# A graph network on one core: new order and timing of the first loads, and x1 + z·h summed ahead of the candidate state in five groups instead of two

## The chip, the cores and the metric

The kernel runs on one core of a Trainium2 chip. A core has a matrix engine (TensorE, PE in the profile; its weight loads are listed apart as PEld), a vector engine (VectorE, DVE), a scalar engine (ScalarE, ACT), GpSimd (POOL) and SyncE (SP), which here issues the DMAs. Each engine runs its instructions in program order and waits on semaphores for the others. The metric is the time of one execution on the device, in microseconds. Before the change it was 2103.77 us, the median of three runs (2102.31 to 2104.01).

## The reference

128 graphs have 128 nodes each, with 256 features per node. Each graph has its adjacency matrix of integers. Two residual layers follow one another; cut to what matters:

```python
# layer 0: three rounds of a gated graph convolution
h = maximum(layernorm(x), 0)
A = (adj != 0)
for i in range(3):
    m = h @ weight[i]                       # [b, n, 256]
    aggr = einsum('bst,bsd->btd', A, m)     # sums over edges
    gi = aggr @ w_ih.T + b_ih;  gh = h @ w_hh.T + b_hh
    r = sigmoid(i_r + h_r);  z = sigmoid(i_z + h_z)
    n = tanh(i_n + r * h_n)                 # the candidate state
    h = (1 - z) * n + z * h
x = x + h
# layer 1: attention over the edges
h = maximum(layernorm(x), 0)
Wh = h @ W;  s = Wh.sum(-1)
e = where(adj == 0, -inf, leaky_relu(s_i + s_j, 0.2))
x = x + softmax(e) @ Wh
```

## The kernel before, in words

The graphs are worked in 32 groups of four (G = 4, NG = 32). A group passes four stages: normalization, and then the three rounds ("layers" 0, 1, 2) of the gated convolution; behind layer 2 follows its attention. In layers 0 and 1 the state is held transposed (hT: features on the partitions); in layer 2 it is held by rows (rows: nodes on the partitions), because the result is added to x, which is kept by rows in the buffer x1.

The product with weight[i] is folded into w_ih ahead of time: the kernel multiplies each weight[i] by w_ih once, at the start (L449, "compose"), so that a round needs only the sum over edges of h (buffer aT) and one product of it. For this w_ih, w_hh and weight are loaded and turned on PE (L351 for w_ih and w_hh, L438 for weight), copied from PSUM to SBUF by DVE and ACT (L358), and their block sums are made (L369 to L377), since the large products use a scheme with seven block multiplications in place of eight. That scheme gives the PSUM banks their names: x_rz, x_n, y_rz, y_n, q_rz, q_n, one bank of each, and two more called misc. The lines L693 and L700 are its matmuls, L732 and L736 to L738 the ACT copies that empty an x or y bank, L725 the ACT copies that seed one, and L742 the DVE additions that read a q bank. A bank is free for its next product only when its copy is done.

The program isn't written in the order in which it runs. Every operation is recorded in a plan (function op) with its engine, an estimated duration, what it reads and writes, a due time and a lag (the time the plan allows from its end until another engine can use the result; 3300 ns for a load). A list scheduler (Plan.run) then ranks the operations by due time, follows clocks for the five engines, and gives out one fixed order for each engine. The operations of PE that belong to the products form a chain of fixed order. The whole is laid out in 96 turns, one for each group and layer, one turn every 18150 ns of planned time (SLOT); in the middle of the kernel each period of three turns takes group g through layer 0, group g−1 through layer 1 and group g−2 through layer 2. The last twelve turns have an order of their own, written out by hand: (29,0), (30,0), (28,1), (27,2), (31,0), (29,1), (28,2), (30,1), (31,1), (29,2), (30,2), (31,2). Because due times and estimated durations decide the order, an edit of one of them can move operations that it doesn't name.

What the change touches:

- L313 to L318: before the planned work, PE runs matmuls of the identity matrix into the banks y_rz and y_n (L315). They write the banks once and are PE's first work. The identity itself is made by POOL (masks.py:197 and 199).
- load (L332 to L334): one DMA on SP's queue, with a lag of 3300 ns. The planner knows no bandwidth of its own: a load costs its size times a constant.
- weights (L387 to L402 and on): the loads of w_ih in two halves of 384 KB (L394 to L397), of weight[0] (load_msg(0), 256 KB), w_hh (768 KB), weight[1] and the biases, each with a due time that ranks it among SP's other issues. In the profile w_ih and w_hh are called rz, since they lie in buffers of that name, and the weights of a layer are called e.
- group (L901 to L906): the loads of a group's rows (512 KB) and adjacency (at, 256 KB). For the first four groups (TIMED = 4) they go through load; later ones are planned with a small fixed cost. L907 turns at into a mask on DVE; L500 to L512 are the statistics of a normalization and L516 its relu on ACT; L530 turns h on PE.
- gru_rows (L819 to L882), the gated update of layer 2. The group's rows are done in two halves. With rz holding tanh(./2), so that z = (rz + 1)/2, a half normally does: the tanh of u on ACT (L855), d = rows − u on DVE (L873), x1 += u on POOL (L875), d = (rz + 1)·d on DVE (L878), and x1 += d/2 on DVE (L881). For the last EARLY_Z groups it does instead, with the same result: d = (rz + 1)·rows (L859) and x1 += d/2 (L862) on DVE, which don't need the candidate state; then the tanh (L855), u = (rz − 1)·u (L865) and x1 −= u/2 (L868), both on DVE. Before, EARLY_Z is 2: groups 30 and 31.

Of the kernel before, what the change touches and what calls it, by code (L numbers as in the profile page):

```python
# [9 lines left out]
BF16 = mybir.dt.bfloat16  # L10
# [6 lines left out]
P = 128  # L17
# [4 lines left out]
WHOLE = 1  # L22
EARLY = 3
ENDING = 2
EARLY_Z = 2
SLOT = 18150
MARGIN = 7000
TIMED = 4
KB = 3
# [12 lines left out]
class Plan:  # L42
# [14 lines left out]
    def buf(self, tag):  # L57
        n, kind = self.tags[tag]
        if kind == "free" or kind == "turn":
            b = Buf(tag, tag, None)  # L60
            if kind == "turn":
                self.waiting.setdefault(tag, []).append((self.phase, len(self.waiting.get(tag, ())), b))
            return b
        key = (tag, self.group % SETS if kind == "set" else 0)
        uses = self.last.setdefault(key, [])
        b = Buf(tag, key, uses[-n] if len(uses) >= n else None)
        b.slot = (key[1], len(uses) % n)
        uses.append(b)
        return b

    def op(self, eng, ns, fn, reads=(), writes=(), room=(), due=None, mark=None,
           turn=None, two=False, lag=None):

        i, deps = len(self.nodes), set()
        for b in room:
            if b.prev is not None:
                deps.update(a[0] for a in b.prev.accesses)  # L80
        for is_write, group in ((False, reads), (True, writes)):
            for item in group:
                b, lo, hi = item if isinstance(item, tuple) else (item, 0, 1 << 30)
                for j, w, l, h in b.accesses:
                    if (w or is_write) and l < hi and lo < h:
                        deps.add(j)
                if is_write and b.prev is not None:
                    deps.update(a[0] for a in b.prev.accesses)
        for is_write, group in ((False, reads), (True, writes)):
            for item in group:  # L90
                b, lo, hi = item if isinstance(item, tuple) else (item, 0, 1 << 30)
                b.accesses.append((i, is_write, lo, hi))
        deps.discard(i)
        bufs = {id(x[0] if isinstance(x, tuple) else x): (x[0] if isinstance(x, tuple) else x)
                for x in list(reads) + list(writes) + list(room)}
        free = [b for b in bufs.values() if self.tags[b.tag][1] in ("free", "turn")]
        for b in free:
            b.users.append(i)
            b.left += 1
        self.nodes.append([eng, ns, fn, deps, free, self.due if due is None else due,  # L100
                           two or eng == "POOL", self.LAG[eng] if lag is None else lag])
        if due is not None:
            self.chain.append(i)
        if mark is not None:
            self.marks[mark] = i
        if turn is not None:
            self.turns.append((i, turn))
# [108 lines left out]
def kernel(  # L216
# [21 lines left out]
    nc = tc.nc  # L238
# [4 lines left out]
    GN = G * N  # L243
# [3 lines left out]
    const = ctx.enter_context(tc.tile_pool(name="const", bufs=1))  # L247
# [39 lines left out]
    phys = {}  # L287
# [9 lines left out]
    def ap(b):  # L297
        return phys[(b.tag,) + b.slot]

    plan = Plan({t: v[:2] for t, v in BUFS.items()})  # L300
    op, buf = plan.op, plan.buf

    ident = const.tile([P, P], F32, name="ident")
# [5 lines left out]

    for kind in ("y_rz", "y_n"):
        y = phys[kind, 0, 0].rearrange("p q n -> p (q n)")  # L313
        for c in range(GN // P):
            nc.tensor.matmul(y[:, c * P:(c + 1) * P], ident, ident, start=(c == 0), stop=True,  # L315
                             skip_group_check=True)


    W = {t: buf(t) for t in ("s_hh", "s_x0", "s_x1", "s_x2", "bias_i", "bias_h", "bias_s", "bias_n", "seed_x",
# [9 lines left out]
        plan.group = SETS - 1  # L329
        return buf(tag)  # L330

    def load(dst, get, src, kb, behind=()):  # L332

        op("SP", kb * KB, lambda: nc.sync.dma_start(get(dst), src), behind, [dst], lag=3300)  # L334

    def plain(b):
        t = ap(b)
# [42 lines left out]
    def weights():  # L380
# [7 lines left out]
        def load_msg(layer, behind=()):  # L388
            load(w_msg[layer], square, weight[layer].rearrange("(k p) e -> p k e", p=P), 256,
                 behind)  # L390


        plan.due = -10 ** 9
        for a in range(2):  # L394
            part = slice(3 * a, 3 * a + 3)
            op("SP", 384 * KB, lambda part=part: nc.sync.dma_start(
                nat(w_ih_nat)[:, part], w_ih.rearrange("(c p) e -> p c e", p=P)[:, part]),  # L397
               [], [(w_ih_nat, a, a + 1)], lag=3300)
        load_msg(0)
        plan.due = 10 ** 9  # L400
        load(w_hh_nat, nat, w_hh.rearrange("(c p) e -> p c e", p=P), 768)
        plan.due = -10 ** 8  # L402
# [60 lines left out]
        for t, i, b in ((tmp[0], 0, b_ih), (tmp[1], 0, b_hh), (tmp[2], 0, b_hh), (tmp[2], 1, b_ih)):  # L463
            n = t is tmp[2]
# [30 lines left out]
    def normed(src, dst, lo=0, hi=G):  # L495

        st, mv, rs, nm = buf("st"), buf("mv"), buf("rs"), buf("nm")
        part = slice(lo, hi)
        for b in range(lo, hi):
            op("DVE", 415, lambda b=b: nc.vector.bn_stats(ap(st)[:, b, :], ap(src)[:, b, :]),  # L500
               [(src, b, b + 1)], [(st, b, b + 1)])

        def aggr():
            for b in range(lo, hi):
                nc.vector.bn_aggr(ap(mv)[:, b, :], ap(st)[:, b, :])
        op("DVE", 160 * (hi - lo), aggr, [st], [mv])

        def rstd():
            nc.gpsimd.tensor_tensor(ap(rs)[:, part], ap(mv)[:, part, 1], eps[:, part], OP.add)
            nc.gpsimd.tensor_tensor(ap(rs)[:, part], ap(rs)[:, part], neghalf[:, part], OP.pow)  # L510
        op("POOL", 1300, rstd, [mv], [rs])
        op("DVE", 170, lambda: nc.vector.scalar_tensor_tensor(  # L512
            ap(nm)[:, part], ap(mv)[:, part, 0], -1.0, ap(rs)[:, part], op0=OP.mult, op1=OP.mult),
           [mv, rs], [nm])
        for b in range(lo, hi):
            op("ACT", 520, lambda b=b: nc.scalar.activation(  # L516
                ap(dst)[:, b, :], ap(src)[:, b, :], AF.Relu, bias=ap(nm)[:, b:b + 1],
                scale=ap(rs)[:, b:b + 1]), [(src, b, b + 1), rs, nm], [(dst, b, b + 1)])
# [306 lines left out]
    def gru_rows(layer, hT, hs, aT, gs, rows, x1):  # L825
# [23 lines left out]
        for n in (1, 0):  # L849
# [3 lines left out]
            def part(b, lo=lo, hi=hi):  # L853
                return ap(b)[:, lo:hi, :].rearrange("p g d -> p (g d)")
            tanh = [723, lambda cols=cols: nc.scalar.activation(  # L855
                ap(u)[:, cols], ap(u)[:, cols], AF.Tanh), [], [(u, lo, hi)]]
            if plan.group >= NG - EARLY_Z:

# [34 lines left out]
    def phase(g, layer):  # L893
        return turns.index((g, layer))

    def group(g):
        graphs = slice(g * G, (g + 1) * G)
        plan.phase = phase(g, 0)
        plan.due = (plan.phase - 1) * SLOT
        rows0, at, a, hT = buf("rows"), buf("at"), buf("a"), buf("hT")  # L900
        for t, src, kb in ((rows0, x[graphs].rearrange("b n d -> n b d"), 512),  # L901
                           (at, adj[graphs].rearrange("b n m -> n b m"), 256)):
            if g < TIMED:
                load(t, ap, src, kb)
            else:
                op("SP", 100, lambda t=t, src=src: nc.sync.dma_start(ap(t), src), [], [t])  # L906
        op("DVE", 420, lambda: nc.vector.tensor_scalar(ap(a), ap(at), 0.0, None,  # L907
                                                       op0=OP.not_equal), [at], [a])
        plan.due = (phase(g, L - 1) + 2) * SLOT
        normed(rows0, rows0)  # L910
        for layer in range(L):
            plan.phase = phase(g, layer)
            if layer == 0:
                if g < EARLY:
                    rows_to_T(rows0, hT)
                else:
                    turned_halves(rows0, True, hT)
                parts = parts_of(rows0) if g >= WHOLE else (rows0, buf("r1"))
            elif layer < L - 1:
                parts = turned_parts(hT)  # L920
            else:
                rows, x1, h1 = buf("rows"), buf("x1"), buf("h1")
                turned_halves(hT, False, rows)
                parts = parts_of(rows)
                op("SP", 100, lambda: nc.sync.dma_start(
                    ap(x1), x[graphs].rearrange("b n d -> n b d")), [], [x1])
            hs, aT, gs = buf("hs"), buf("aT"), buf("gs")
            node_sums(hT, hs, "POOL", 1390, 940)
            edge_sums(parts, a, aT)
            node_sums(aT, gs, "DVE", 690, 440)  # L930
            plan.cursor = plan.phase * SLOT
            if layer < L - 1:
                gru(layer, hT, hs, aT, gs)
        plan.due = min(phase(g, L - 1) + 3, len(turns) + 0.5) * SLOT
        gru_rows(L - 1, hT, hs, aT, gs, rows, x1)
        if g < NG - 1:
            attention(g, lambda: edges_of(g, a), x1, h1, 0, G)
        else:
            scores = edges_of(g, a)
            for lo, hi in ((G // 2, G), (0, G // 2)):  # L940
                attention(g, lambda: scores, x1, h1, lo, hi)
# [216 lines left out]
    for g in range(NG):  # L1158
        plan.group = g
        group(g)  # L1160
# [31 lines left out]
```

## Time and profile before

| | before |
|---|---|
| median of three runs | 2103.77 us |
| the profiled execution | 2105.1 us |
| its span (first to last instruction) | 2102.2 us |
| PE busy | 2087.1 us, 99% of the span |
| DVE busy | 1667.5 us, 79% |
| ACT busy | 1591.4 us, 76% |
| POOL busy | 938.8 us, 45% |
| one period of three turns in the middle (start of a y_rz product to the same one a period later: 1156.34 to 1220.47) | 64.13 us |
| operations of layer 2's update | L875 60 times, L859 4 times |

A line of a timeline or of the table of groups gives the start and duration in microseconds, the engine, the line of the program, the operation, its output and its inputs by the program's names, and the shape; what stands in brackets is how long the engine had been idle before it, and what released it. An idle time is charged to the instruction that came last by the profile. A line of the stretches gives the busy time of each engine in one stretch of the span, with the number of instructions. "PEclk" is the clock that PE was granted, as a share of full speed.

### The profile page before, as it was taken

The page shows a single profiled execution, that of the slowest core. Times are in us where ns is not written, and L with a number is a line of the kernel's source. Part 1 is how long each engine was busy: PE and PEld are TensorE (multiplying, and loading weights), DVE is VectorE, ACT ScalarE, POOL GpSimd, SP SyncE. Part 2 cuts the span into 40 slices and gives each one's busy share as a digit, 9 for nine tenths or more (in the row PEclk, how much of TensorE's full clock was granted, in tenths as well). Part 3 has the DMA queues.
Part 4 walks back from the last instruction along what each step waited for, and adds up shares of the span by engine and source line. Part 5 has one row for each costly group of instructions (what it writes and reads, how often), then busy time and mean ns, then how long its engine had stood idle before and what let it go on. Part 6 is the DMA issues. An engine that isn't in the chain of part 4 may idle for free.

```text
span 2102.2 us, 33964 instructions
## 1 busy us (share of the span) xinstructions
PE 2087.1 (99%) x12430; PEld 1864.0 (89%) x12430; DVE 1667.5 (79%) x3369; ACT 1591.4 (76%) x2849; POOL 938.8 (45%) x881
## 2 busy tenths in 40 slices
PE   8999999999999999999999999999999999999998
PEld 7888888898888998898988889988989888988887
DVE  6767888887877788777888777887778887778778
ACT  5567878777877777777778787777777787777676
POOL 4544554445543444544354434444343544335330
PEclk9999999999999999999999999999999999999999
DMA  4222223222233222332222332223332223223331
GB/s 131 61 51 52 54 52 77 69 51 67 68 74 76 51 62 64 71 81 66 52 65 68 73 76 51 65 64 68 81 66 59 58 63 78 56 51 51 75 76 36
DMA packets 365158, 137.21 MB, mean 65 GB/s; under 512 B 296384, under 2 KB 364736, under 8 KB 364992
## 3 DMA queue, kind: packets, MB, share of 16 engines
q1 hardware_dynamic: 364992, 135.05, 28.5%
q8 instruction: 97, 1.59, 0.3%
q14 instruction: 69, 0.57, 0.1%
HBM read 45.36 MB, written 16.78 MB: 30 GB/s over the span
## 4 chain that ended last, share of the span: by engine, by line
PE 97%; DVE 2%; ACT 1%; DMA 0%; issue 0%; SPq 0%; DVEq 0%
PE y_rz L693 16%; PE q_rz L693 11%; PE x_rz L693 10%; PE y_n L693 8%; PE y_rz L700 8%; PE misc L620 6%; PE x_n L693 5%; PE q_n L693 5%; PE q_rz L700 5%; PE x_rz L700 5%; PE misc L1076 5%; PE y_n L700 4%; PE x_n L700 3%; PE q_n L700 3%; PE misc L649 2%; DMA at<-in_adj_dram 0%
## 5 line engine op out<-in xcount | busy, mean ns | idle before, releaser
L577 POOL TENSOR_TENSOR r<-rows 128x512 f32<-128x512 f32 x126 | 136.3, 1102 | 270.8 <-ACT rows L560 183.6
L732 ACT COPY t_rz<-y_rz 128x512 f32<-128x512 f32 x192 | 112.4, 585 | 180.8 <-PE y_rz L693 91.9
L602 POOL TENSOR_TENSOR pl<-d,pl 128x512 bf16<-128x512 f32 x64 | 74.9, 1173 | 296.3 <-ACT pl L600 296.1
L742 DVE TENSOR_TENSOR t_rz<-t_rz,q_rz 128x512 f32<-128x512 f32 x192 | 131.2, 684 | 94.2 <-ACT t_rz L732 54.2
L693 PE MATMUL y_rz<-hs,s_hh 128*128 128x256 f32 x768 | 197.5, 380 | 0.0
L693 PE MATMUL y_rz<-gs,s_x 128*128 128x256 f32 x768 | 197.1, 379 | 0.0
L667 POOL TENSOR_TENSOR hs<-hT,hs 128x256 f32<-128x256 f32 x96 | 81.9, 853 | 239.6 <-PE q_n L700 171.8
L663 POOL TENSOR_TENSOR hs<-hT 128x512 f32<-128x512 f32 x96 | 130.4, 1358 | 98.7 <-ACT hT L560 32.1
L693 PEld LDWEIGHTS y_rz<-gs,s_x 128*128 128x128 f32 x768 | 145.9, 190 | 19.8
L693 PEld LDWEIGHTS y_rz<-hs,s_hh 128*128 128x128 f32 x768 | 143.1, 190 | 18.8 <-issue 0.5
L580 POOL TENSOR_TENSOR p<-r 128x512 bf16<-128x512 f32 x126 | 154.2, 1243 | 0.0
L742 DVE TENSOR_TENSOR t_n<-t_n,q_n 128x512 f32<-128x512 f32 x192 | 131.2, 683 | 20.9 <-ACT t_n L732 8.6
L693 PE MATMUL x_rz<-hT,s_hh 128*128 128x256 f32 x512 | 131.5, 379 | 0.0
L693 PE MATMUL x_rz<-aT,s_x 128*128 128x256 f32 x512 | 131.4, 379 | 0.0
L500 DVE BATCH_NORM_STATS2 st<-rows 128x6 f32<-128x256 f32 x128 | 45.2, 413 | 96.8 <-DMA rows<-in_x_dram 96.8
L623 ACT COPY aT<-misc 128x512 f32<-128x512 f32 x190 | 110.5, 584 | 13.3 <-PE misc L620 9.4
L815 DVE TENSOR_TENSOR d<-hT,u 128x512 f32<-128x512 f32 x128 | 109.8, 858 | 9.6 <-ACT u L812 9.5
L693 PE MATMUL y_n<-hs,s_hh 128*128 128x256 f32 x384 | 114.4, 379 | 0.0
L693 PE MATMUL y_n<-gs,s_x 128*128 128x256 f32 x384 | 114.2, 379 | 0.0
L1076 PE MATMUL misc<-w,uT 128*128 128x256 f32 x480 | 113.3, 380 | 0.3 <-ACT uT L654 0.3
L597 POOL TENSOR_TENSOR d<-hT,pl 128x512 f32<-128x512 f32 x64 | 90.7, 1418 | 51.4 <-ACT pl L595 45.6
L693 PEld LDWEIGHTS x_rz<-aT,s_x 128*128 128x128 f32 x512 | 97.2, 190 | 13.2
(277 smaller groups left out, 6503.6 us busy)
## 6 DMA issues: line engine op xcount, KB each, us to landing
rows<-in_x_dram SPq DMA_DIRECT2D x32, 512.0 KB, 4.1
x<-in_x_dram SPq DMA_DIRECT2D x32, 512.0 KB, 3.9
out_dram<-x SPq DMA_DIRECT2D x31, 512.0 KB, 2.9
at<-in_adj_dram SPq DMA_DIRECT2D x32, 256.0 KB, 2.8
plT<-pl SPq DMA_TRANSPOSE x186, 3.3
peT<-pe SPq DMA_TRANSPOSE x60, 3.1
rz<-in_L_gnn_w_ih_dram SPq DMA_DIRECT2D x2, 384.0 KB, 3.6
e<-in_L_gnn_weight_dram SPq DMA_DIRECT2D x3, 256.0 KB, 6.1
```

The lines of the kernel that those rows point to most:

```text
L577: op("POOL", 1106, lambda part=part: nc.gpsimd.tensor_tensor(ap(r1)[:, part], ap(rows)[:, part], top(rows)[:, part], OP.subtract), [(rows, ...
L580: op("POOL", 1050, lambda part=part: nc.gpsimd.tensor_tensor(ap(p3)[:, part], ap(r1)[:, part], top(r1)[:, part], OP.subtract), [(r1, n, n ...
L597: op("POOL", 1150, lambda k=k, r=r: nc.gpsimd.tensor_tensor(ap(r), ap(hT)[:, k], part(pl, k, 0), OP.subtract), [(hT, 2 * k, 2 * k + 2), (p ...
L620: nc.tensor.matmul(flat(ps)[:, b * N:(b + 1) * N], part(i, b, k), ap(a)[:, b, :], start=(i == 0), stop=(i == 2))
L623: op("ACT", 590, lambda k=k, ps=ps: nc.scalar.copy(ap(dst)[:, k, :], flat(ps)), [ps], [(dst, 2 * k, 2 * k + 2)])
L663: op(eng, cost, lambda: sub(ap(w)[:, 0:2, :], blocks()[:, 1::2, :], blocks()[:, 0:2, :], OP.subtract), [t], [(w, 0, 2)], two=True)
L693: nc.tensor.matmul(ap(bank)[:, half, :], ap(w)[:, i - 1, q, :], source(t, sums), start=(first and c == 0 and m == 0), stop=False, skip_gro ...
L700: nc.tensor.matmul(ap(bank)[:, m, half * P:(half + len(chunk)) * P], source(t, sums)[:, m * N:(m + 1) * N], ap(w)[:, i - 1, q:q + len(chun ...
L732: op("ACT", 590, lambda: nc.scalar.copy(ap(t), ap(y)), [y], [t], mark=mark)
L742: op("DVE", 690, lambda: nc.vector.tensor_tensor(ap(t), ap(t), ap(q), OP.add), [q], [t])
L815: op("DVE", 690, lambda j=j, d=d, cols=cols: nc.vector.tensor_tensor(ap(d), ap(hT)[:, j, :], ap(u)[:, cols], OP.subtract), [(hT, lo, hi), ...
L1076: nc.tensor.matmul(ap(ps)[:, b, :], ap(uT)[:, k, (m + b) * N:(m + b + 1) * N], ap(w1)[:, k, :], start=(k == 0), stop=(k == KD - 1))
```

## The change

Three edits:

- PE's first matmuls. In place of eight fp32 products of the identity with itself, a tile of zeros (128 x 512, bf16) is set by DVE, and one bf16 matmul per bank, 512 columns wide, writes y_rz and y_n.
- The order of the first loads. weight[0] is given a due time ahead of everything, so it is the first DMA on SP's queue, ahead of the two halves of w_ih. The adjacency of the first four groups is planned with a lag of 4800 ns rather than 3300, so that it is issued earlier; for this load takes the lag as a parameter. The order on SP's queue was: w_ih (two halves), weight[0], weight[1], rows of group 0, w_hh, at of group 0, rows of group 1. It is now: weight[0], w_ih (two halves), weight[1], rows, at, w_hh, rows of group 1.
- EARLY_Z is 5, not 2: groups 27, 28 and 29 also sum x1 + z·h ahead of the tanh. This also moves operations of DVE, ACT and POOL in other groups, since the planner places all of them; the order on PE differs in the first 320 us or so and in the last turns, and is the same in between.

```diff
-EARLY_Z = 2
+EARLY_Z = 5
...
+    zeros = const.tile([P, GN], BF16, name="zeros")
+    nc.vector.memset(zeros, 0.0)
     for kind in ("y_rz", "y_n"):
-        y = phys[kind, 0, 0].rearrange("p q n -> p (q n)")
-        for c in range(GN // P):
-            nc.tensor.matmul(y[:, c * P:(c + 1) * P], ident, ident, start=(c == 0), stop=True,
-                             skip_group_check=True)
+        nc.tensor.matmul(phys[kind, 0, 0].rearrange("p q n -> p (q n)"), zeros[:, :P], zeros, start=True,
+                         stop=True, skip_group_check=True)
...
-    def load(dst, get, src, kb, behind=()):
-
-        op("SP", kb * KB, lambda: nc.sync.dma_start(get(dst), src), behind, [dst], lag=3300)
+    def load(dst, get, src, kb, behind=(), lag=3300):
+
+        op("SP", kb * KB, lambda: nc.sync.dma_start(get(dst), src), behind, [dst], lag=lag)
...
+        plan.due = -2 * 10 ** 9
+        load_msg(0)
         plan.due = -10 ** 9
         for a in range(2):
             part = slice(3 * a, 3 * a + 3)
             op("SP", 384 * KB, lambda part=part: nc.sync.dma_start(
                 nat(w_ih_nat)[:, part], w_ih.rearrange("(c p) e -> p c e", p=P)[:, part]),
                [], [(w_ih_nat, a, a + 1)], lag=3300)
-        load_msg(0)
...
             if g < TIMED:
-                load(t, ap, src, kb)
+                load(t, ap, src, kb, lag=4800 if t is at else 3300)
```

## The prediction

> **What bounds the kernel.** I read the busy totals and the chain of waits first, then TensorE's (PE's) busy time by stretches, then PE's waits, and last the timeline around each wait.
>
> ```profile
> PE 2087.1 (99%) x12430; PEld 1864.0 (89%) x12430; DVE 1667.5 (79%) x3369; ACT 1591.4 (76%) x2849; POOL 938.8 (45%) x881
> PE 97%; DVE 2%; ACT 1%; DMA 0%; issue 0%; SPq 0%; DVEq 0%
> ```
>
> PE is busy 99% and is 97% of the chain. Only removed matmuls or removed PE gaps can shorten the span; the other engines count only where they open a gap. Stretches say where the gaps are:
>
> ```profile
> 0.00:100.00 100.00, 93.74 (x516) 78.41 (x517) 71.03 (x138) 59.58 (x122) 56.32 (x62) 1.00 0.38 101
> 1900.00:2000.00 100.00, 100.00 (x590) 89.23 (x589) 78.36 (x142) 68.15 (x125) 47.68 (x44) 1.00 0.32 65
> 2000.00:2100.00 100.00, 95.04 (x586) 84.11 (x584) 80.58 (x199) 70.64 (x139) 20.39 (x22) 1.00 0.19 51
> ```
>
> Columns: stretch, length, busy us (instructions) of PE, its weight loads, DVE, ACT, POOL, then clock, DMA share, GB/s. From 300 to 2000 us PE is full in every stretch. Idle are 6.3 us at the head, 0.36 + 1.36 = 1.72 us from 198 to 203, and, of the last 100 us, 3.4 us in gaps before PE's last work at 2098.46 (the rest follows it). The largest waits:
>
> ```profile
> PE y_rz L700 <- ACT t_rz L732: 2.8, 2, 1.5
> PE misc L438 <- DMA e<-in_L_gnn_weight_dram: 1.8, 1, 1.8
> PE y_rz L315 <- POOL ident masks.py:199: 1.4, 1, 1.4
> PE misc L449 <- DVE h L358: 0.9, 1, 0.9
> PE misc L530 <- DVE h L358: 0.8, 1, 0.8
> ```
>
> (total, times, longest.) The profiled execution took 2105.1 us, span 2102.2 and 2.9 outside it: 1.3 above the median of 2103.77. I work in differences and apply them to the median.
>
> **What the skill says.** "TensorE: Matmul & The Clock Gate", Part 1, "What's actually happening": PE starts at half clock and is released after a busy window of about 3.4 us, whose phase is free. The trace agrees: the first 8 warm-up records advance 1.87 us (1.36 to 3.23), 234 ns each; transposes from 4.70 advance 110 ns each. Part 4 says transposes don't count as busy in the same way; nothing in this trace tests that. "SBUF — State Buffer", "Who interferes with whom": a DVE operation with two SBUF inputs and a POOL operation that reads SBUF exclude each other. The trace agrees: L873, 0.68 us at the median, took 1.76 beside L875. "DMA: Bandwidth & Descriptors", "Queues, rings and completion order": an engine takes descriptors in ring order[...]. It agrees: e0 is third in the queue and lands at 7.83.
>
> **Part 1, warm-up.** Removed: 8 fp32 matmuls, 16 records, 3.5 us (1.36 to 4.86). Added: a DVE memset of 512 bf16 and two bf16 matmuls of 512 columns. The page's 1.2 GHz gives an estimated 0.43 us each, about 0.9 in all, from about 1.0. The 2.6 us saved is not on the path: PE then waits for a load. What may be lost is the warm clock, as 0.9 us can't fill a 3.4 us window.
>
> **Part 2, loads.** The same bytes go out on the one SP queue, in the order e0, w_ih halves, e1, rows, adjacency (at), w_hh, rather than w_ih halves, e0, e1, rows, w_hh, at. SP takes about 0.5 us an issue. Before, landings were w_ih 4.02 and 5.12, e0 7.83, e1 8.56, rows 10.06, w_hh 12.34, at 13.17. By bytes ahead I estimate now: e0 3.65, w_ih 4.5 and about 7.7 (it inherits the stretch of 5 to 7 us in which part of the engines stalled), e1 8.56, rows 10.06, at about 10.8, w_hh about 13.2. PE's first composition of weights (L449) starts at 9.16 before and needs e0 and all of w_ih; in the new PE order it also stands behind e1's four transposes. So it starts at about 9.2: no gain, whatever happens to the 1.79 us wait. PE then does four compositions of layer 0 (about 5.2 us: 1.7 per 512 columns, half that per 256) until 14.4, the w_hh transposes (1.3) and one composition of layer 1 (1.7) until 17.5–18.0, where the first transposes of h (L530) started at 18.21. w_hh arriving 0.8 later is covered by the compositions; if they were shorter it would cost that 0.8. at arriving 2.4 earlier frees DVE, which waited 0.48 for it (L907 at 13.19) with the copies of the compositions (L358) behind it. So the 0.94 gap at 24.60 and the 0.80 gap at 29.25, both waits for L358, shrink. I expect −0.7 to −1.3 at full clock. At half clock until 12 us or so, 3.4 us of composition takes up to 1.7 more, partly regained in the gaps: net +1.5 at the worst. Taken: **−0.7**.
>
> **The order from 190 to 206 us** shifts too: the q_n seed wait (0.36) goes, but the q_rz seed now stands behind both aT copies on ACT (about 1.2 late), and the t_rz copy ends at about 203.3 against 203.4. Bounds −1.7 to +1.5, taken 0.
>
> **Part 3, x1 + z·h ahead of tanh in groups 27 to 29** (30 and 31 did it already). Per half, L875 on POOL (1.28 us) goes; L873, L878 and L881 on DVE (0.68, 0.69, 0.69) become four operations (L859, L862, L865, L868, of 0.68 to 0.69). For 6 halves that is 6 × 0.69 = +4.1 us DVE and −6 × 1.28 = −7.7 us POOL. The DVE time is hidden: DVE is 78% busy from 1900 to 2000, and PE has no gap there; in a full stretch such as 2030 to 2040 (DVE 9.77 of 10) it would cost up to its 0.69 each.
>
> The gain sits in one gap. In the timeline of the last turns:
>
> ```profile
> 2032.39 1.39 POOL L875 TENSOR_TENSOR x<-x,u 128x512 f32<-128x512 f32 x1 [2.93 <-ACT u L855]
> 2032.56 1.76 DVE L873 TENSOR_TENSOR d<-rows,u 128x512 f32<-128x512 f32 x1
> 2036.22 1.53 DVE L881 SCALAR_TENSOR_TENSOR x<-d,x 128x512 f32<-128x512 f32 x1
> 2042.52 2.08 ACT L516 ACTIVATE h<-x,nm,rs 128x256 f32<-128x256 f32 x4 [5.52 <-DVE nm L512]
> 2044.50 0.56 ACT L732 COPY t_rz<-y_rz 128x512 f32<-128x512 f32 x1
> 2045.11 1.13 PE L700 MATMUL y_rz<-s_hh,hs 128*128 128x256 f32 x4 [1.47 <-ACT t_rz L732]
> ```
>
> The copy that frees y_rz stands on ACT behind the four relus L516 of group 29, which waited 5.52 us for its x1. With z·h summed early, no L875 and neither 1.76 nor 1.53 of collision, nm comes some 2.5 to 4 us earlier (2037.5 to 2039 against 2042.48). The relus are then done by 2041, before PE ends y_rz at about 2042.8, and the copy runs when PE is ready. The 1.47 goes; a copy without delay still takes 0.56, and today's other work hides that. The small gaps near it (0.33 at 2034.0, 0.28 at 2059.9) may go. Next late: the tanhs of group 30, now behind the y_n copy. From the last attention's L1108 on, the order is unchanged. Bounds −2.1 to 0; taken **−1.6**.
>
> **The middle, 300 to 2000 us.** PE's order is unchanged, but the planner re-sorts DVE, ACT and POOL in each of some 23 periods of 64.1 us. For example L855 goes ahead of a copy L732. PE has no gap there, so there is nothing to gain. To lose: the tightest y_rz block starts 0.97 us after its copy L732 ended. A tanh of 0.63 before it stays inside that. Bounds 0 to +9 (0.4 × 23); taken **+0.2**.
>
> Sum: −0.7 + 0 − 1.6 + 0.2 = −2.1; 2103.77 − 2.1 = **2101.7**.
>
> **Rivals.**
> *Half clock* (0.15): the short warm-up leaves PE cold through the compositions. For: 0.9 us of work, then idle until 3.65, then transposes. Against: the phase is free, and waits hide part. Head +1.5 for −0.7: about 2103.9.
> *Nothing arrives* (0.12): landings follow total bytes and the tail's wait moves to the next copy: about 2103.5.
> *A new stall in every period* (0.17), on the slow side: the re-sorted ACT queue delays the copy L732 before y_rz. It decides from a delay of 0.97 us: each 0.1 beyond costs 2.3 over 23 periods, and 0.3 costs 7, so 2103.77 − 2.3 + 7 = 2108.5. For: DVE operations beside POOL take 1.5 to 1.8 for 0.69, so one new collision uses the margin. Against: most blocks have 1.5 us or more.
> *All of it* (0.14): head −1.8, 190 to 206 −1.7, tail −2.1: 2098.2.
> The forecast has 0.42.
>
> **Range and chances.** A measurement of this kernel tells about 0.2%, 4.2 us, from no change. Faster (under 2099.6): "all of it" and a few hundredths of the forecast, 0.17. Slower (over 2108.0): most of the stall case, 0.15. Within: 0.68. The range 2097.6 to 2108.4 reaches to both. The forecast's own is 2100.2 to 2103.2.
>
> **What would show it.** Right: the wait on e at L438 under 0.5 and an earlier at, L907 without its 13.17; no 1.47 before y_rz near 2044; L875 54 times, not 60, and L859 10, not 4; PE full from 300 to 2000. Wrong: transposes over 200 ns apart after 5 us, or compositions at double length (half clock); PE idle once per 64 us (stall); a wait on L732 or on another copy between 2035 and 2065 (tail). A stall in the middle would break the forecast most, since it is multiplied by 23.

## The result

The changed kernel takes 2118.38 us, median of four runs (2116.9 to 2119.53), against 2103.79 for the kernel before. The ratio is 1.0068, with a 95% interval of 1.0056 to 1.0080. It is 14.6 us slower; I had forecast 2.1 us faster. The profiled execution took 2116.9 us, with a span of 2115.0 against 2102.2.

The page of the changed kernel, its busy totals and its chain (line numbers behind the edits are one higher than before):

```profile
PE 2092.8 (99%) x12416; PEld 1860.4 (88%) x12416; DVE 1706.8 (81%) x3376; ACT 1588.4 (75%) x2849; POOL 934.7 (44%) x875
PE 76%; DVE 16%; ACT 5%; issue 2%; DMA 0%; DVEq 0%; SPq 0%; ACTq 0%
```

PE still reads 99%, but the chain that ended last is only 76% PE, where it was 97%: it now leaves PE for DVE and ACT over and over. DVE is busy 39 us longer. The edit adds only seven DVE instructions (3369 to 3376): a memset and the six operations that I had priced at 4.1 us. So instructions that were there before got longer. The stretches and the waits of PE say where:

```profile
300.00:400.00 100.00, 99.75 (x600) 89.48 (x598) 82.20 (x156) 78.22 (x141) 45.78 (x42) 1.00 0.32 61
1000.00:1100.00 100.00, 99.47 (x596) 88.45 (x595) 84.12 (x159) 77.23 (x141) 47.36 (x43) 1.00 0.28 62
2000.00:2100.00 100.00, 98.10 (x615) 88.50 (x614) 81.41 (x178) 71.05 (x130) 20.86 (x21) 1.00 0.18 43
```

```profile
PE misc L650 <- ACT aT L624: 6.8, 22, 0.8
PE misc L439 <- DMA e<-in_L_gnn_weight_dram: 1.4, 1, 1.4
...
PE q_rz L701 <- ACT q_rz L726: 1.2, 1, 1.2
PE y_n L694 <- ACT t_n L733: 1.1, 1, 1.1
PE y_rz L701 <- ACT t_rz L733: 1.0, 2, 0.7
PE misc L621 <- POOL p L581: 1.0, 1, 1.0
```

The middle, where PE had no gap at all, now has 22 waits of one kind, one in each period from 386 to 1745 us: the attention's matmuls L650 (L649 before) wait for the ACT copy L624 that empties a misc bank. Twenty of them show 0.25 to 0.27 us each, two show 0.78 and 0.85.

The idle time shown is only half of what such a wait costs. I compared the starts of the y_rz products in both traces: each of the twenty waits moves everything behind it by 0.53 us, and the last two by 1.04 and 1.12. (Steps of 0.84 to 0.89 us, which come from the order of PE itself, are left out: there are four of them from 283 to 390 us, and they are undone in the last turns.) Of the 0.53, 0.43 is the later start of L650, and 0.10 more is lost inside its eight matmuls. The rest of the start's delay hides in the modelled end of the matmuls ahead. Sum: 20 × 0.53 + 1.04 + 1.12 = 12.8 us.

The whole account in the two spans, by the same comparison: −1.22 at the first y_rz product near 32 us; −0.32 near 200; +12.8 in the middle; and the remaining +1.6 behind it. The last matmul ends 12.79 later (2098.46 to 2111.25).

What delays the copy can be read in one period. Timeline of the kernel before, at one of these places:

```profile
825.04 0.50 ACT L806 ACTIVATE rz<-t_rz,bias_s 128x256 f32<-128x256 f32 x1
...
827.53 0.42 DVE L803 SCALAR_TENSOR_TENSOR u<-u,y_n 128x256 f32<-128x256 f32 x1
827.99 0.72 ACT L812 ACTIVATE u<-u,bias_i 128x512 f32<-128x512 f32 x1
828.00 1.16 POOL L602 TENSOR_TENSOR pl<-d,pl 128x512 bf16<-128x512 f32 x1 [2.79 <-ACT pl L600]
828.47 0.68 DVE L742 TENSOR_TENSOR t_n<-t_n,q_n 128x512 f32<-128x512 f32 x1
...
830.95 0.57 ACT L623 COPY aT<-misc 128x512 f32<-128x512 f32 x1
...
833.01 1.05 PE L649 MATMUL misc<-eT,h 128*128 128x128 f32 x8
```

The same place in the changed kernel, 5.58 us later by PE's q_rz product just ahead (832.09 before, 837.67 now):

```profile
830.37 1.15 POOL L603 TENSOR_TENSOR pl<-d,pl 128x512 bf16<-128x512 f32 x1 [1.66 <-ACT pl L601]
830.56 1.51 DVE L822 SCALAR_TENSOR_TENSOR hT<-d,u 128x512 f32<-128x512 f32 x1
...
832.80 1.15 POOL L598 TENSOR_TENSOR d<-hT,pl 128x512 f32<-128x512 f32 x1
832.97 1.26 DVE L804 SCALAR_TENSOR_TENSOR u<-u,t_n 128x256 f32<-128x256 f32 x1
...
835.05 0.72 ACT L813 ACTIVATE u<-u,bias_i 128x512 f32<-128x512 f32 x1 [2.33 <-DVE u L804]
835.68 0.49 ACT L807 ACTIVATE rz<-t_rz,bias_s 128x256 f32<-128x256 f32 x1
...
838.40 0.57 ACT L624 COPY aT<-misc 128x512 f32<-128x512 f32 x1
...
839.02 1.16 PE L650 MATMUL misc<-eT,h 128*128 128x128 f32 x8 [0.27 <-ACT aT L624]
```

Before, L602 on POOL ran beside L742, which reads one of its two inputs from a PSUM bank and kept its 0.68 us. Now POOL's two operations that split the state (L603, L598) run about 3 us earlier against PE, beside L822 and L804. These have both inputs in SBUF, and take 1.51 for 0.69 and 1.26 for 0.42. That fits the Trainium skill, "SBUF — State Buffer", "Who interferes with whom": a DVE operation with two SBUF inputs contends with a POOL operation that reads SBUF, and one with at most one SBUF input, outside the modes that take both ports, doesn't. The kernel before has such collisions as well (L803 takes 1.27 at 830.65 beside L597), but behind this tanh. The tanh L813 waits for the chain of which L804 is part and starts 1.48 later against PE. One more activation, L807 at 835.68, now runs between the tanh and the copy; before, it ran at 825.04, ahead of the tanh. It adds 0.39, so the copy ends 1.87 later (838.97 − 831.52 − 5.58). Its margin before was 833.01 − 831.52 = 1.49. The excess, 0.38, and some 0.05 from copy to PE, is the 0.43.

### The profile page after: what moved, and what is told of

It reads as the page before. It is cut to its first block, busy times and chain, and to the rows that moved or that the text cites. A ratio compares the mean times of both kernels' runs of the same rounds, so it can differ in the third digit from the quotient of the medians.

```text
span 2115.0 us, 33825 instructions
## 1 busy us (share of the span) xinstructions
PE 2092.8 (99%) x12416; PEld 1860.4 (88%) x12416; DVE 1706.8 (81%) x3376; ACT 1588.4 (75%) x2849; POOL 934.7 (44%) x875
## 4 chain that ended last, share of the span: by engine, by line
PE 76%; DVE 16%; ACT 5%; issue 2%; DMA 0%; DVEq 0%; SPq 0%; ACTq 0%
PE y_rz L694 11%; PE x_rz L694 9%; PE y_rz L701 8%; PE q_rz L694 7%; PE y_n L694 5%; PE misc L1077 5%; PE misc L621 5%; PE x_n L694 4%; PE q_rz L701 4%; PE y_n L701 4%; PE q_n L694 4%; PE x_rz L701 4%; PE q_n L701 3%; DVE d L816 3%; DVE d L819 2%
## 5 line engine op out<-in xcount | busy, mean ns | idle before, releaser
L664 POOL TENSOR_TENSOR hs<-hT 128x512 f32<-128x512 f32 x96 | 137.2, 1429 | 175.7 <-PE y_n L701 103.3
L603 POOL TENSOR_TENSOR pl<-d,pl 128x512 bf16<-128x512 f32 x64 | 79.7, 1249 | 285.2 <-ACT pl L601 285.0
L668 POOL TENSOR_TENSOR hs<-hT,hs 128x256 f32<-128x256 f32 x96 | 87.8, 915 | 236.4 <-PE q_n L701 176.8
L816 DVE TENSOR_TENSOR d<-hT,u 128x512 f32<-128x512 f32 x128 | 139.0, 1086 | 26.9 <-ACT u L813 26.7
L581 POOL TENSOR_TENSOR p<-r 128x512 bf16<-128x512 f32 x126 | 148.7, 1199 | 0.0
L813 ACT ACTIVATE u<-u,bias_i 128x512 f32<-128x512 f32 x128 | 92.5, 723 | 61.3 <-DVE u L804 61.3
L664 DVE TENSOR_TENSOR gs<-aT 128x512 f32<-128x512 f32 x96 | 101.8, 1061 | 37.9 <-ACT aT L624 37.3
L624 ACT COPY aT<-misc 128x512 f32<-128x512 f32 x190 | 109.8, 582 | 27.2 <-PE misc L621 24.1
L819 DVE SCALAR_TENSOR_TENSOR d<-rz,d 128x512 f32<-128x512 f32 x128 | 111.8, 873 | 4.7
L822 DVE SCALAR_TENSOR_TENSOR hT<-d,u 128x512 f32<-128x512 f32 x128 | 110.9, 866 | 3.3
```

The source lines that it names most:

```text
L581: op("POOL", 1050, lambda part=part: nc.gpsimd.tensor_tensor(ap(p3)[:, part], ap(r1)[:, part], top(r1)[:, part], OP.subtract), [(r1, n, n ...
L624: op("ACT", 590, lambda k=k, ps=ps: nc.scalar.copy(ap(dst)[:, k, :], flat(ps)), [ps], [(dst, 2 * k, 2 * k + 2)])
L664: op(eng, cost, lambda: sub(ap(w)[:, 0:2, :], blocks()[:, 1::2, :], blocks()[:, 0:2, :], OP.subtract), [t], [(w, 0, 2)], two=True)
L816: op("DVE", 690, lambda j=j, d=d, cols=cols: nc.vector.tensor_tensor(ap(d), ap(hT)[:, j, :], ap(u)[:, cols], OP.subtract), [(hT, lo, hi), ...
L819: op("DVE", 690, lambda d=d, cols=cols: nc.vector.scalar_tensor_tensor(ap(d), ap(rz)[:, 1, cols], 1.0, ap(d), op0=OP.add, op1=OP.mult), [( ...
L822: op("DVE", 690, lambda j=j, d=d, cols=cols: nc.vector.scalar_tensor_tensor(ap(hT)[:, j, :], ap(d), 0.5, ap(u)[:, cols], op0=OP.mult, op1= ...
```

## The experiments

**Why the order in the middle changed.** EARLY_Z edits only groups 27 to 29, at the end. But the planner ranks each operation by the work that hangs on it, backward from the end. The path that ranked all the products, in the planner's numbers (engine, line, planned ns), ran from the last products of group 29's layer 2 through that group's update to its softmax, which has a fixed early place:

```
before:  ... ACT L855 723 -> POOL L875 1290 (+300 lag) -> DVE L881 690 -> DVE L500 -> ... -> exp L1042
after:   ... ACT L855 723 -> DVE  L865  690            -> DVE L868 690 -> DVE L500 -> ... -> exp L1042
```

The new path is 1290 + 300 − 690 = 900 ns shorter. So nearly every product, with what feeds it, became 900 ns less urgent, while the x1 work and the attention kept their ranks. That reorders ACT, DVE and POOL from the first groups on. I call this the rank theory.

Four kernels test it. One has only the last edit:

```diff
-EARLY_Z = 2
+EARLY_Z = 5
```

> EARLY_Z = 5 alone; warm-up and loads as before. Rank theory (taking L875 out of group 29 shortens a planned path by 900 ns, which moves the rank of every product and its feeders back to the start of the kernel, and the new order of ACT, DVE and POOL stalls PE before the attention's alpha.h matmuls once per 64 us): about +15 us, 2116 to 2120, with about 20 waits of L649 on the copy L623. Load theory (the new order of loads shifts the buffers and phases that the middle inherits): no such waits, 2101 to 2104. DVE theory (the six added DVE operations in groups 27 to 29 cost the time): slower by at most 4 us, all of it after 1880 us.

Measured: 2119.15 against 2104.07, ratio 1.0075 (1.0059 to 1.0090), with the same 22 waits. One has the other edits without it:

```diff
 EARLY_Z = 2
+    zeros = const.tile([P, GN], BF16, name="zeros")
...
+        plan.due = -2 * 10 ** 9
+        load_msg(0)
...
+                load(t, ap, src, kb, lag=4800 if t is at else 3300)
```

> Warm-up, load order and lag of at as changed; EARLY_Z = 2. Rank theory: the middle is as before, PE full from 300 to 2000 us, and the head keeps the 1.2 us that the changed kernel had gained by 32 us: 2102.0 to 2103.2 against 2103.8. Load theory: slower by 10 to 13 us, with the waits of L649. DVE theory: as the rank theory.

Measured: 2103.97 against 2104.07, ratio 1.0001 (0.9993 to 1.0009). PE is full in the middle, and the last matmul of the profiled execution ends 1.33 earlier. In the median this gain isn't seen; the kernels of the head, below, come back to it. The third leaves all instructions of the kernel before as they are and changes one planned number:

```diff
-            op("POOL", 1290, lambda cols=cols, part=part: nc.gpsimd.tensor_tensor(
+            op("POOL", 390 if plan.group == NG - 3 else 1290, lambda cols=cols, part=part: nc.gpsimd.tensor_tensor(
```

> The kernel before, with one number of the plan changed: L875 of group 29 is planned as 390 ns, not 1290 ns. No instruction is added, removed or changed, only their order. Rank theory: about 20 to 22 waits of L649 on L623 of 0.26 to 0.8 us, each 0.53 us or more in effect: +11 to +14 us, 2114 to 2118. Load theory and DVE theory: 2103 to 2105.

Measured: 2118.25, ratio 1.0069 (1.0055 to 1.0083). Its waits of PE begin:

```profile
PE misc L649 <- ACT aT L623: 6.7, 22, 0.8
```

No operation was added, and none took another engine: the order alone costs the 14 us. The last puts the 900 ns back on the path of the whole change:

```diff
-                op("ACT", *tanh)
+                op("ACT", *tanh, lag=1200 if plan.group < NG - 2 else None)
```

> The whole change, but the tanh L855 of groups 27 to 29 is planned with a lag of 1200 ns in place of 300, which puts the 900 ns back on the planned path; the instructions issued are the same. Rank theory: the middle is as before, no waits at L649, and the gains of the head (1.2 to 1.5) and of the tail (1 to 2) are left: 2100.3 to 2102.0. Load theory and DVE theory: as slow as the changed kernel, 2115 to 2119 (load), or 1 to 4 us slower than before (DVE).

Measured: 2107.01, ratio 1.0014 (1.0007 to 1.0020). The 22 waits are gone, as the rank theory said, and 11 us are back. But this kernel, the held one from here on, is 2.9 us slower than the kernel before, not 2 to 4 faster: that miss is taken up below. The load theory and the DVE theory fall with these four.

**How large must the shift be?** The same number, 1250 in place of 1290.

> The kernel before, with L875 of group 29 planned as 1250 ns in place of 1290: the ranks move by 40 ns, not 900. The planner gives the same new order in the middle as with 900. If the order is what costs, the time is that of the kernel with 900: 2116 to 2119, about 20 waits of L649. If the size of the shift counts (less of the margin used), 2104 to 2106.

Measured: 2118.63, ratio 1.0071 (1.0057 to 1.0085), with the same 22 waits of 6.7 us in all. A planned time 40 ns shorter costs as much as one 900 ns shorter. In the ranks, the two lie closer together than the expectation says. With L875 at 390 ns, the path by L873, L878 and L881 (3 × 690 = 2070 ns) takes over from the one by L875 (1290 + 300 + 690 = 2280 ns), so the ranks of the products moved by 210 ns there, and by 40 ns here. In every kernel run here, DVE and ACT have one of two orders in the middle, and the price is that of the order, not of the shift.

**What in the new order delays the copy.** The changed kernel, with less work in two POOL operations and everything else in its place (the first of the two is shown):

```diff
-            op("POOL", 1150, lambda k=k, r=r: nc.gpsimd.tensor_tensor(
-                ap(r), ap(hT)[:, k], part(pl, k, 0), OP.subtract),
+            op("POOL", 1150, lambda k=k, r=r, c=slice(0, 32 if plan.group >= 4 else GN): nc.gpsimd.tensor_tensor(
+                ap(r)[:, c], ap(hT)[:, k, c], part(pl, k, 0)[:, c], OP.subtract),
```

> The changed kernel; from group 4 on the two POOL operations that split the state for its transposes (L598, L603) work on 32 columns of 512, so their planes hold old numbers. The plan and the order of all engines are those of the changed kernel. Collision theory (these two now run beside DVE's u chain and L822 and hold it up by 1.5 to 1.7 us; the tanh L813 that waits for it delays the copy L624 behind it on ACT): the waits of L650 on L624 go, 12 to 13 us are back, 2104 to 2107. Queue theory (it is enough that one more activation, L807, stands ahead of the copy L624): the waits stay, 2115 to 2119.

Measured: 2103.37 against 2104.12, ratio 0.9998 (0.9990 to 1.0006): 15.0 us less than the changed kernel, and no wait of L650 is left in the middle. At the same place (first the POOL operation, then the DVE operation that it had held up, and the tanh):

```profile
827.38 0.69 DVE L822 SCALAR_TENSOR_TENSOR hT<-d,u 128x512 f32<-128x512 f32 x1
827.42 0.75 POOL L603 TENSOR_TENSOR pl<-d,pl 128x32 bf16<-128x32 f32 x1 [1.89 <-ACT pl L601]
...
830.14 0.72 ACT L813 ACTIVATE u<-u,bias_i 128x512 f32<-128x512 f32 x1 [0.60 <-DVE u L804]
```

L822 is back at 0.69, and the tanh waits 0.60 for DVE, not 2.33. The activation L807 stays between the tanh and the copy (at 830.77), so the queue alone doesn't make the wait. By the sum above the collisions alone wouldn't either: of the delay of 1.87, they make 1.48 and L807 0.39, against a margin of 1.49. No kernel here keeps the collisions and takes L807 away, so this second half is worked out, not tested. The shorter POOL operations also let POOL's later work start earlier, which this kernel doesn't separate from the collisions. The time is 0.6 us under the range expected: the waits at 1890 and 1968 went too.

**The head.** The two edits of the head apart, with EARLY_Z = 2. The loads:

```diff
+        plan.due = -2 * 10 ** 9
+        load_msg(0)
...
-        load_msg(0)
...
+                load(t, ap, src, kb, lag=4800 if t is at else 3300)
```

> The new order of loads and the lag of at, with the eight identity matmuls per kernel kept as before and EARLY_Z = 2. Clock theory (the head of the changed kernel gains by its loads, and its two short matmuls give part of that back in those executions in which PE stays at half clock into the compositions): PE at full clock from 4.5 us, the first large product 1.3 to 2 us earlier in every execution, 2101.5 to 2102.8. If the warm-up is of no account: as with all edits of the head, 2104.0.

Measured: 2103.02 against 2104.12, ratio 0.9997 (0.9989 to 1.0005). The warm-up:

```diff
-        for c in range(GN // P):
-            nc.tensor.matmul(y[:, c * P:(c + 1) * P], ident, ident, start=(c == 0), stop=True,
-                             skip_group_check=True)
+        nc.tensor.matmul(phys[kind, 0, 0].rearrange("p q n -> p (q n)"), zeros[:, :P], zeros, start=True,
+                         stop=True, skip_group_check=True)
```

> The two zero matmuls in place of the eight of the identity, nothing else. Clock theory: PE at half clock until somewhere between 7 and 13 us; the transposes of w_ih and weight[0] and, in part of the executions, the compositions run at half speed: 2104.3 to 2106.5 and more scatter. If the warm-up is of no account: 2103.5 to 2104.3.

Measured: 2104.10, ratio 1.0003 (0.9994 to 1.0011). Both intervals include 1, so by their times the two edits of the head are not told from nothing, and the clock theory's ranges are missed, each by 0.2 us. In the profiled executions the loads bring every later product forward by 1.13 us, and the zeros move them by 0.03. The half clock is there, though. The first composition, in the changed kernel and in the held one:

```profile
8.46 1.03 PE L450 MATMUL x_rz<-x,uT 128*128 128x256 f32 x4
```

```profile
9.50 1.91 PE L450 MATMUL x_rz<-x,uT 128*128 128x256 f32 x4
```

In the held kernel's profiled execution PE stayed at half clock into the second composition, to about 11.7 us, and the first y_rz product came 0.95 later than before, not 1.2 to 1.3 earlier. The changed kernel, with the same head, had the clock at 7.3. With the identity warm-up kept, the last slow product or transpose with the identity lies between 4.1 and 6.9 us in nine profiles; with the zeros, between 6.4 and 9.1 in five, and in two of those five compositions ran slow. So the risk of the short warm-up is real, but falls on part of the executions, and runs of one kernel spread over 1 to 5 us anyway.

**The end.** In the held kernel a new wait of 2.02 us stands before q_rz, where there had been 1.47 before y_rz. Behind it the granted clock (third figure from the end) falls to half for 3.4 us:

```profile
2042.36 1.80 PE L701 MATMUL q_rz<-s_x,gs 128*128 128x256 f32 x4 [2.02 <-DVE gs L664]
```

```profile
2042.70:2046.10 3.40, 3.40 (x14) 3.04 (x13) 2.85 (x10) 1.14 (x2) 0.50 (x1) 0.50 0.45 143
2046.10:2050.00 3.90, 3.90 (x23) 3.54 (x22) 0.00 (x0) 1.26 (x3) 0.00 (x0) 1.00 0.62 162
```

So the miss has two parts in this execution: 0.95 us at the head, and 2.43 us more by the last matmul, which ends 3.38 later than before. Of its 21 executions, the 11 with a mean granted clock of 0.999 have a median of 2108.00 us, the 10 with 1.000 one of 2105.14.

Two kernels narrow it down: the new loads with the identity warm-up, the lag of 1200, and EARLY_Z = 3:

```diff
-EARLY_Z = 2
+EARLY_Z = 3
```

> New order of loads with the identity warm-up kept; EARLY_Z = 3 (group 29 alone is new) with the tanh of that group planned at a lag of 1200 ns, so that the middle and PE's whole order stay as before. Step of the prediction under test: the 1.47 us wait before y_rz near 2044 goes, since the relus L516 of group 29 no longer wait for L875 and L881. If that step holds: no gap over 0.4 us between 2030 and 2060, the last matmul about 1.3 earlier than in the loads-alone kernel, 2100.6 to 2102.0. If the wait moves to another copy or another queue, as in the held kernel: 2102.5 to 2104.

and the same with EARLY_Z = 4:

> The same with EARLY_Z = 4 (groups 28 and 29). If the step holds: as with group 29 alone, 2100.6 to 2102.0, since there is no gap at group 28 to gain. If each group moved early crowds DVE at the end: slower than group 29 alone by 0.5 to 2.

Measured: 2105.32 and 2105.64 against 2104.19, ratios 1.0006 (0.9997 to 1.0014) and 1.0007 (0.9999 to 1.0016). The 1.47 is gone in both, and both have the new wait, of 2.21 us. With groups 28 and 29 the clock falls behind it as in the held kernel (0.51 from 2042.4 to 2045.9); with group 29 alone it keeps 1.00 in the profiled execution. From 2011 us to the last matmul, the one with the fall loses 2.53 us against the kernel before, the one without it 1.38. Why the clock falls after one wait of 2.21 us and not after another isn't shown. Timeline of the kernel with group 29 alone:

```profile
2038.84 0.98 DVE L513 SCALAR_TENSOR_TENSOR nm<-mv,rs 128x4 f32<-128x4 f32 x1
2039.74 0.47 DVE L1086 SCALAR_TENSOR_TENSOR x<-misc,rden,x 128x256 f32<-128x256 f32 x1
2040.14 1.21 DVE L664 TENSOR_TENSOR gs<-aT 128x512 f32<-128x512 f32 x1
...
2041.40 1.13 PE L701 MATMUL q_rz<-s_x,gs 128*128 128x256 f32 x4 [2.21 <-DVE gs L664]
```

In the kernel before, the sum L663 ran at 2035.63, ahead of all this. Now group 29's x1 is early, its more urgent normalization is ready first, and L664 of group 30 stands behind it in DVE's queue: behind nm, which waits for POOL, and L1086, which waits for PE. So two last kernels take those sums first, with EARLY_Z = 3 and 5:

```diff
+            summed = len(plan.nodes)
             node_sums(aT, gs, "DVE", 690, 440)
+            if (g, layer) == (NG - 2, L - 1):
+                plan.first = range(summed, len(plan.nodes))
...
+        for i in self.first:
+            rank[i] = -float("inf")
```

> As with group 29 alone held, and the three DVE sums L664 to L668 of group 30's last layer are taken ahead of any other ready DVE work. If the 2.2 us wait of q_rz on L664 in the held kernels is only that sum's place in DVE's queue, behind the x1 work of group 29: the wait goes, the 1.47 wait before y_rz stays away, and the tail is 1 to 2 us shorter than that of the kernel before: 2101.0 to 2102.5. If the end has no slack on DVE and the wait only moves again: 2102.5 to 2105.

> The same with EARLY_Z = 5, as in the changed kernel. If the wait is only a place in the queue: 2101.0 to 2102.5. If it moves again: 2102.5 to 2105.

Measured: 2103.53 and 2103.66 against 2104.17, ratios 0.9997 (0.9989 to 1.0005) and 0.9998 (0.9990 to 1.0006). The 2.2 goes and some 1.8 us come back, but no gain can be told. 1.17 us now stand before q_rz on its seed L725 near 2057; even so, in the profiled executions the last y_rz product starts 0.89 and 0.84 us earlier than in the kernel before, when the head is taken off. The last turn then takes it away. From that product to the last matmul the kernel before needs 25.88 us and these two 27.31, among it 0.68 before L649 near 2081. Their PE order in this stretch isn't that of the kernel before, but that of the two kernels with one planned number changed, which need 27.31 there as well. So the tail has a gain, and the planner's order of the last turn costs more than it. No kernel here is told from the kernel before on the fast side.

## Why the prediction was wrong

**The middle: the step that failed.** The prediction saw that the planner re-sorts three engines in every period, and took +0.2, with bounds of 0 to +9. It read the margin of one kind of place only: "the tightest y_rz block starts 0.97 us after its copy L732 ended". The place that gave way was another, the misc bank before L649. Its margin was larger, 1.49 us; but the delay that came was 1.87, not "a tanh of 0.63". The middle measured +12.8 us.

The slow rival had the mechanism: a DVE operation beside POOL uses up the margin of a copy on ACT, and the wait repeats each period. It named the wrong bank and priced the wait at 0.3 us; 0.53 was measured. The range ended 10 us too low. Its upper bound took 0.4 us per period, with no measurement behind it.

What the prediction had no step for is why the order moved at all: it priced L875's removal where L875 ran, not in the plan, where it stood on the path that ranks everything.

**The end** was taken as −1.6, and measured +1.6 behind the middle. The 1.47 wait did go, as forecast. New waits came in the changed kernel: 1.09 before y_n at 1890, 0.74 before y_rz at 1968, 0.58 and 1.02 before L621 at 2053. "Next late" was asked, and answered with the tanhs; it was group 30's sums on DVE in the held kernels, and seeds, copies and another order of the last turn elsewhere. Half clock behind such a wait had no place in the prediction. The forecast that nm comes 2.5 to 4 us earlier held in the kernel with group 29 alone: 2038.84 + 0.98 = 2039.82 against 2042.48, in an execution that stood within 0.1 us of the kernel before until 1968. What comes early also takes its place in a queue early: that was the missing half of the step.

**The head** was taken as −0.7 and measured −1.22 in this execution, within "−0.7 to −1.3", but in part by other steps than those named, so the number is partly luck. The loads landed in the order of their issue, but from the second half of w_ih on some 1.2 us earlier than estimated (this half at 6.54, not 7.7), and the composition began at 8.46: 0.70 earlier than before, where "no gain" had been said. The 0.94 gap at 24.6 is gone, as forecast, but the wait before the transposes of h (L530), which was to shrink, grew from 0.80 to 1.34. The wait on e, which was to fall under 0.5, is 1.43; it stands before transposes that begin at 3.71 rather than 7.96, so as a sign it told little. The half-clock rival shows in part of the executions.

**190 to 206** was taken as 0 and measured −0.32. The q_rz seed cost 1.17, as forecast; the q_n wait of 0.36 went, and the y_rz wait shrank from 1.36 to 0.30.

**The DVE time of the six operations** was hidden, as far as can be seen: the kernel with the small POOL operations has all six, and from 210 us to its last matmul it takes 0.64 us less than the kernel before. Its POOL operations are shorter there too, so this isn't a measure of the six alone.

## What to carry to other kernels

Where a planner ranks work backward from the end, an edit of the last groups is an edit of all groups if it stands on the ranking path: compare the order of every engine in the steady part, not only of the bottleneck's, and hold the old order (here by a planned lag) to see what the edit itself is worth. In a steady part at 99%, list the margin of every bank that is handed back, and set it against the sum of what can pile up ahead of the copy: DVE operations held up by POOL, and each activation moved ahead. A recurring wait cost twice its idle time here; take the cost from the period between like instructions.

## What was not expected of the hardware

- A quarter microsecond of idle PE before eight matmuls stood for 0.53 us lost, in each of twenty periods.
- A DVE operation with two SBUF inputs ended 0.55 and 0.28 us after the POOL operation that had started 0.2 us ahead of it: 1.51 and 1.26 us for 0.69 and 0.42. One with an input in PSUM kept 0.68 beside the same POOL operation.
- Transposes released PE's clock: with the zeros as the only edit, PE did nothing but transposes between the two zero matmuls, which end at 2.28 us, and the compositions from 9.16. Those from 4.23 to 7.03 us advanced 0.21 us each, those from 7.97 on 0.11 to 0.14, waits aside. The Trainium skill, "TensorE: Matmul & The Clock Gate", Part 4, says that they don't count as busy in the same way; here the measurement decides.
- Behind a PE wait of 2.02 us, and behind one of 2.21 in another kernel, PE had half clock for 3.4 us, in the middle of dense work; behind a second wait of 2.21 it hadn't.
